# Convolution of a stage in two parts, batch statistics by ScalarE, one product of two blocks, and B and C by two transfers

## The chip, the core and the metric

The kernel runs on one core of a Trainium2 chip. TensorE (PE) multiplies matrices, VectorE (DVE) and GpSimd (POOL) do element-wise work, ScalarE (ACT) evaluates functions with a scale and a bias, SyncE (SP) issues transfers, and 16 DMA engines carry them. The metric is the device time of one execution in microseconds. Everything is in fp32.

## The reference, cut to what matters

The input x is 32 images of 96 channels, 56x56 each. It passes a ConvNeXt block (a depthwise 7x7 convolution, a LayerNorm, an MLP with GELU, a residual), then two Mamba layers over the 3136 tokens of an image, then a fused projection with a batch-norm over all images.

```python
# ConvNeXt block
h = conv_general_dilated(x, conv_w, padding=((3,3),(3,3)), feature_group_count=dim) + conv_b
...                                        # LayerNorm, w1, GELU, w2, scale
x = h + x
# a Mamba layer
dbl = xc @ xproj_w                         # dt (6), B (16), C (16) of each token
delta = softplus(dt @ dt_w + dt_b)         # 192 channels
dA  = exp(delta[..., None] * A)
dBx = delta[..., None] * Bm[:, :, None, :] * xc[..., None]
hstates = associative_scan(...)            # h[t] = dA[t] * h[t-1] + dBx[t], 192 x 16 rows
y = einsum('blds,bls->bld', hstates, Cm) + Dp * xc
y = y * silu(z)
...
# the end
out = einsum('oc,bchw->bohw', fus_w, cat) + fus_b
mu, var = out.mean((0, 2, 3)), out.var((0, 2, 3))
out = (out - mu) * rsqrt(var + EPS) * bn_g + bn_b
return out + residual
```

## The kernel before, in words

After a setup (to about 640 us) that also convolves the images of the first group of batches, a main loop runs 256 **stages**: 2 layers x 32 images x 4 chunks of 784 tokens (CH; half of it, 392, is HC). The order alternates the layers, so that a chunk of layer 2 follows soon after its layer 1. A final pass (from 17140 us) normalises and writes the output in 64 tiles.

A stage holds 192 x 16 scans of 784 tokens. They are done 128 rows at a time: 6 blocks j of 32 channels, times 4 groups g of 4 states, which gives 24 **steps**. A step consists of these instructions:

- ACT computes dA as an exp of the d tile (L805). A d tile has 128 rows: four copies of 32 channels of delta, brought by four transfers (load_d4, L684).
- PE spreads u (delta times xc) of a block over the 128 rows (spread, L820), and DVE multiplies it with B (w, L847). For the two "pooled" blocks, j = 2 and 5, POOL does this product instead (L831), from a tile us which transfers bring (L675).
- DVE runs the scan (L854); POOL multiplies with C (L858); PE adds up over the states (add_up, L885 and L891).
- Three times a stage DVE multiplies y with the gate (L872).

B and C come by transfer: the 32 rows of dbl go to a DRAM tile bd (dbl_out), and load_bc brings, for each group g, a tile bc of 128 partitions x 2 x 784: partitions 32s to 32s+31 hold 32 copies of the rows of B and C of state 4g+s. There are 8 such buffers, and a stage uses four.

All other work is cut into **pieces** that have a slot: a number whose whole part is the step after which the piece is put into the instruction stream, and whose fraction is its order there. A piece marked True runs within a step, between w and the scan. `prep` holds the pieces for the next stage (projections of the Mamba layer, dbl, softplus, the product u, loads of bc, d and us); its slots are counted for the coming stage and begin with negative ones. `post` ends the stage before: project (7.5), then two halves of move from PSUM (9 and 10), and in layer 2 the statistics for the batch-norm with DVE's bn_stats (stat, L760, at 13 within a step), after which the half is saved to o_d. `block0` is half a tile of the ConvNeXt block, and `conv` one channel pair of the depthwise convolution for a group of seven images: as a matrix product with a banded matrix over 112 rows (2 channels x 56), one product per horizontal tap. It is in 144 of the stages (stages 2 to 145). PSUM tiles from psum(0), psum(1) and psum(2) have one buffer each.

The order on every engine is written out by hand this way: each engine, and SP's queue of transfers too, executes its instructions in that order and waits at the head for what is not ready. The program's transfers share a few completion semaphores in turn, so that only some are under way at a time. The final pass reads the statistics back, merges them (bn_aggr, L967), and scales all tiles.

Of the kernel before, what the change touches and what calls it, by code (L numbers as in the profile page):

```python
# [34 lines left out]
F32 = mybir.dt.float32  # L35
I32 = mybir.dt.int32
AF = mybir.ActivationFunctionType
ALU = mybir.AluOpType
AX = mybir.AxisListType
# [4 lines left out]
L = H * W  # L44
C = 96
DIN = 192
NQ = 3
NS = 16
# [3 lines left out]
NCH = 4  # L52
CH = L // NCH
HC = CH // 2
# [7 lines left out]
def convnext_mamba_kernel(  # L62
# [31 lines left out]
    nc = tc.nc  # L94
    B = x.shape[0]

    dram = ctx.enter_context(tc.tile_pool(name="dram", bufs=1, space=DRAM))
# [3 lines left out]
    NB = 7  # L101
    b0 = B - 3 * NB if B > 3 * NB else B
    groups = [(0, b0)] + [(b, b + NB) for b in range(b0, B, NB)]
    conv_d = [
        dram.tile([C * H, (hi - lo) * W], F32, name=f"conv_d{lo}", tag=f"conv_d{lo}")
        for lo, hi in groups
    ]
    band_d = dram.tile([C // 2, 2 * H, 7 * 2 * H], F32, name="band_d")
    stats_d = dram.tile([C, B * NCH, 12], F32, name="stats_d")
    x1_d = [dram.tile([C, L], F32, name=f"x1_d{b}", tag=f"x1_d{b}") for b in range(B)]  # L110
    o_d = [dram.tile([C, L], F32, name=f"o_d{b}", tag=f"o_d{b}") for b in range(B)]

# [82 lines left out]
    for i in range(2):  # L195
# [12 lines left out]
        if i == 1:  # L208

            d["res"] = fw1  # L210
            for q in range(NQ):
                ps = sups.tile([128, 512], F32, name="ps", tag="nps")
# [5 lines left out]
                ps = sups.tile([128, 512], F32, name="ps", tag="nps")  # L218
# [29 lines left out]
    for k in range(2):  # L248
        t = const.tile([C + 1, 3 + CH], F32, name=f"hn{k}", tag=f"hn{k}")
        nc.vector.memset(t[C : C + 1, :], 1.0)  # L250
        hns.append(t)
        t = const.tile([C + 1, HC], F32, name=f"hz{k}", tag=f"hz{k}")
# [4 lines left out]
    R2 = 2 * H  # L257
    GB = (b0 + 1) // 2
    cb = const.tile([R2, C // 2], F32, name="cb")
    with tc.tile_pool(name="cc", bufs=1) as cc, tc.tile_pool(name="cx", bufs=3) as cx, tc.tile_pool(  # L260
        name="cp", bufs=6, space=PSUM
# [31 lines left out]
        for i in range(3):  # L293
            t = cc.tile([R2, 7, R2], F32, name=f"band{i}", tag=f"band{i}")
            nc.gpsimd.memset(t, 0.0)
            bands.append(t)
            t = cc.tile([R2, b0, W + 6], F32, name=f"xpad{i}", tag=f"xpad{i}")
            nc.gpsimd.memset(t, 0.0)
            xpads.append(t)
        for p in range(C // 2):  # L300
# [13 lines left out]
            for lo in range(0, b0, GB):  # L314
                n = min(GB, b0 - lo)
                ps = cps.tile([R2, GB * W], F32, name="ps")
                for dw in range(7):
                    nc.tensor.matmul(
                        ps[:, 0 : n * W], T[:, dw, :], xp[:, lo : lo + n, dw : dw + W],
                        start=(dw == 0), stop=(dw == 6),  # L320
# [3 lines left out]
                    bias=cb[:, p : p + 1],  # L324
# [4 lines left out]
    with ExitStack() as main:  # L329
        wp = main.enter_context(tc.tile_pool(name="wp", bufs=2))  # L330
# [12 lines left out]
        def tok(a):  # L343
            return slice(a * HC, (a + 1) * HC)
# [34 lines left out]
        batch_bias = {}  # L379
# [103 lines left out]
        xpad = wp.tile([R2, NB, W + 6], F32, name="xpad", tag="xpad", bufs=1)  # L483
        nc.vector.memset(xpad, 0.0)

        def conv(g, p):
            lo, hi = groups[g]
            v = {}

            def load():  # L490
                v["band"] = wp.tile([R2, 7, R2], F32, name="band", tag="band", bufs=1)
                nc.sync.dma_start(v["band"].rearrange("p k n -> p (k n)"), band_d[p])
                nc.sync.dma_start(
                    xpad[:, :, 3 : 3 + W],
                    x[lo:hi, 2 * p : 2 * p + 2, :].rearrange("b c (h w) -> (c h) b w", w=W),
                )

            def taps_(dws):
                def piece():
                    if dws[0] == 0:  # L500
                        v["ps"] = psum(2)
                    for dw in dws:
                        nc.tensor.matmul(  # L503
                            v["ps"][0:R2, 0 : NB * W], v["band"][:, dw, :],
                            xpad[:, :, dw : dw + W], start=(dw == 0), stop=(dw == 6),
                        )

                return piece

            def store():  # L510
                t = wp.tile([R2, HC], F32, name="sq", tag="sq", bufs=3)
                nc.scalar.activation(
                    t[:, 0 : NB * W], v["ps"][0:R2, 0 : NB * W], AF.Identity, bias=cb[:, p : p + 1]
                )
                nc.sync.dma_start(conv_d[g][p * R2 : (p + 1) * R2, :], t[:, 0 : NB * W])

            return [
                (-10, load), (7.7, taps_((0,))), (8.2, taps_((1,))), (8.6, taps_((2,))),
                (9.2, taps_((3,))), (9.6, taps_((4,))), (10.2, taps_((5,))), (10.4, taps_((6,))),
                (11.05, store),  # L520
            ]


# [6 lines left out]
        def prep(S):  # L530

            i, b, c = S.i, S.b, S.c
            d = lay[i]
            v = {}
# [81 lines left out]
            def load_bc(gs):  # L616
                def piece():
                    for g in gs:
                        t = wp.tile([128, 2, CH], F32, name="bc", tag="bc", bufs=8)
                        for s in range(4):  # L620
                            nc.sync.dma_start(
                                t[32 * s : 32 * s + 32],
                                v["bd"][4 * g + s :: NS, :].partition_broadcast(32),
                            )
                        S.bcs.append(t)

                return piece
# [20 lines left out]
                    nc.sync.dma_start(ddv[a], dl[rows(a)])  # L648
                S.d4 = []

            def product(q):
                def piece():
                    if q == 0:
                        S.u = wp.tile([128, NQ, HC], F32, name="u", tag="u", bufs=1)
                    nc.gpsimd.tensor_tensor(S.u[:, q], v["dl"][:, q], S.xc[:, q], ALU.mult)  # L655

                return piece

            def store_u(k):
                def piece():  # L660
                    j = POOLED[k]
                    if k == 0:
                        v["uu"] = bcd.tile([len(POOLED), 32, CH], F32, name="uu", tag="uu")
                        S.us = {}
                    for a in range(2):
                        r = 64 * a + 32 * (j % 2)
                        nc.sync.dma_start(v["uu"][k, :, tok(a)], S.u[r : r + 32, j // 2, :])

                return piece
# [10 lines left out]
            def load_d4(j):  # L680
# [11 lines left out]
            start = [  # L692
                (-18, load), (-12.9, center), (-11.9, square), (-11.8, halo), (-11.6, mean),
                (-11.2, root), (-9, True, norm),
            ]
            t = (-7.6, -7.5, -6.5, -6, 0, 0.1, 1, 2.3, 3.1, 3.4, 4)
            if S in (stages[2], stages[-1]):
# [5 lines left out]
                t = (12, 12, 13, 13, 14, 14, 15, 16, 17, 18, 19)  # L703
            elif S is stages[3]:
# [6 lines left out]
            t = [k + 0.1 for k in t]  # L711
# [6 lines left out]
                (t[6] + 0.2, silu("z", None)), (t[7], dbl), (t[8], dbl_out),  # L718
                (max(10.2, t[8] + 1.2), load_bc((0, 1))), (max(13.2, t[8] + 2.2), load_bc((2, 3))),
                (t[9], dt), (t[10], softplus),  # L720
                (max(16.2, t[10] + 1), product(0)), (max(17.2, t[10] + 2), product(1)),
                (max(18.3, t[10] + 3.1), store_u(0)), (25.2, product(2)), (26.3, store_u(1)),
                (max(17, t[10] + 2), load_d4(0)), (max(18, t[10] + 3), load_d4(1)),
                (max(20, t[10] + 3.2), load_u(0)), (23, load_d4(2)),
                (26, load_d4(3)), (32.9, load_u(1)), (30, load_d4(4)), (35, load_d4(5)),
# [2 lines left out]
        def post(S):  # L728


            i, b, c = S.i, S.b, S.c
            v = {}

            def project():
                v["ps"] = [psum(0), psum(1)]
                for a in range(2):
                    nc.tensor.matmul(
                        v["ps"][a][0:C, 0:HC], S.d["res"], S.seq[:, tok(a)],
                        start=True, stop=False,
                    )  # L740
                for q in range(NQ):
                    for a in range(2):
                        nc.tensor.matmul(
                            v["ps"][a][0:C, 0:HC], S.d["ow"][rows(a), q, :], S.z[rows(a), q, :],
                            start=False, stop=(q == NQ - 1),
                        )

            def move(a):
                def piece():
                    nc.scalar.activation(  # L750
                        S.seq[:, tok(a)], v["ps"][a][0:C, 0:HC], AF.Identity,
                        bias=batch_bias[b] if i == 1 else 0.0,
                    )

                return piece

            def stat():
                st = wp.tile([C, 2, 6], F32, name="stat", tag="stat", bufs=2)
                for a in range(2):
                    nc.vector.bn_stats(st[:, a, :], S.seq[:, tok(a)])  # L760
                nc.sync.dma_start(stats_d[:, b * NCH + c, :], st.rearrange("p a k -> p (a k)"))
                nc.sync.dma_start(o_d[b][:, c * CH : (c + 1) * CH], S.seq)
                del seqs[b, c]

            pieces = [(7.5, project), (9, move(0)), (10, move(1))]
            if i == 1:
                pieces.append((13, True, stat))
            return pieces


# [190 lines left out]


    mv = const.tile([C, 2], F32, name="mv")
    with tc.tile_pool(name="sp", bufs=1) as sp:
        stats = sp.tile([C, B * NCH * 2, 6], F32, name="stats")
        nc.sync.dma_start(stats.rearrange("p (n a) k -> p n (a k)", a=2), stats_d)
        nc.vector.bn_aggr(mv, stats)  # L967
    sc = const.tile([C, 1], F32, name="sc")
    nc.scalar.activation(sc, mv[:, 1:2], AF.Sqrt, bias=eps_c[0:C])
    nc.vector.reciprocal(sc, sc)  # L970
# [74 lines left out]
```

## Time and profile before

| | |
|---|---|
| time, median of 3 runs | 17518.44 us (17515.35 to 17520.57) |
| profiled execution | 17504.21 us, its span 17502.5 us |
| granted TensorE clock, mean | 0.936 |
| busy share of the span | DVE 92%, POOL 89%, PE 87%, ACT 64% |
| DMA | 2346.89 MB, mean 134 GB/s; 4096 transfers bc<-bd of 196 KB, 5.2 us to landing |
| first scan / end of the last scan | 641.8 us / 17128.3 us |

A row of a group gives the line, the engine and operation, the tile written and the tiles read, the shapes and the count; then busy time and the mean of one in ns; then the idle time of the engine ahead of it, and what ended that idle time. A window gives for a stretch of time its length and the busy time of each engine in it, with the number of instructions in brackets, then PE's granted clock, the mean busy share of the 16 DMA engines and the GB/s moved. A row of waits gives the engine and what it was about to do, what released it, the total, the number of times and the longest. Times of the DMA rows are medians from issue to landing.

### The profile page before, as it was taken

To read this page: it belongs to the slowest core of one execution; us is meant where nothing else is said; L and a number is where in the kernel's file an instruction comes from. 1 tells how busy PE (TensorE), PEld (TensorE's weight loads), DVE (VectorE), ACT (ScalarE), POOL (GpSimd) and SP (SyncE) were. 2 spreads that over 40 slices of the span, in tenths; PEclk is the share of its full clock that TensorE was granted. 3 is DMA by queue.
4 is the path that set the end of the run, shared out by engine and by line. 5 is a ranking of instruction groups with operands and counts; after the bars stand their busy time and mean duration, and the time that the engine had idled before them with its cause. 6 is when DMAs were issued, how large, how long until landed. Compare 5 with 4: busy or idle time off the path is not lost. (4 is left out here: it accounts for less than half of the span.)

```text
span 17502.5 us, 212206 instructions
## 1 busy us (share of the span) xinstructions
PE 15285.5 (87%) x65976; PEld 5191.4 (30%) x65976; DVE 16171.5 (92%) x12592; ACT 11224.1 (64%) x17479; POOL 15632.4 (89%) x8993
## 2 busy tenths in 40 slices
PE   7799999999999999999999988888888888888880
PEld 5233333333333333333333322222222222222220
DVE  7499999999999999999999999999999999999994
ACT  1566666666666666666666666666666666666653
POOL 0499999999999999999999999999999999999991
PEclk9799999999999999999999999999999999999985
DMA  4355555555555555555555555555555555555548
GB/s 102 87 139 138 138 135 136 140 139 139 138 135 138 137 140 138 134 137 137 139 139 134 136 126 128 128 125 125 126 129 127 125 126 126 129 127 124 126 116 273
DMA packets 1403525, 2346.89 MB, mean 134 GB/s; under 512 B 627654, under 2 KB 775154, under 8 KB 1402388
## 3 DMA queue, kind: packets, MB, share of 16 engines
q1 hardware_dynamic: 1395220, 2294.77, 53.1%
q10 hardware_dynamic: 7168, 38.54, 0.6%
q8 instruction: 520, 8.52, 0.2%
q14 instruction: 617, 5.05, 0.1%
HBM read 1929.50 MB, written 402.80 MB: 133 GB/s over the span
## 5 line engine op out<-in xcount | busy, mean ns | idle before, releaser
L858 POOL TENSOR_TENSOR da<-h,bc 128x784 f32<-128x784 f32 x6144 | 11295.8, 1863 | 884.9 <-DVE h L854 721.8
L854 DVE TENSOR_TENSOR_SCAN h<-da,st,w 128x784 f32<-128x784 f32 x3072 | 5662.4, 1843 | 314.3 <-ACT st L865 8.6
L891 PE MATMUL y<-da,ssum 128*32 128x392 f32 x24576 | 5086.0, 533 | 562.9 <-POOL da L858 561.2
L847 DVE TENSOR_TENSOR w<-w,bc 128x784 f32<-128x784 f32 x4096 | 3996.0, 976 | 311.0 <-PE w L820 139.5
L831 POOL TENSOR_TENSOR da<-us,bc 128x784 f32<-128x784 f32 x2048 | 3818.4, 1864 | 2.3 <-DMA us<-uu 2.3
L805 ACT ACTIVATE da<-d,A 128x784 f32<-128x784 f32 x4096 | 3753.9, 941 | 44.8 <-DMA d<-dd 28.6
L805 ACT ACTIVATE w<-d,A 128x784 f32<-128x784 f32 x2048 | 1879.6, 918 | 2659.7 <-DVE h L854 2403.2
L854 DVE TENSOR_TENSOR_SCAN h<-w,st,da 128x784 f32<-128x784 f32 x1536 | 2712.5, 1827 | 5.7 <-ACT st L865 4.6
L891 PEld LDWEIGHTS y<-da,ssum 128*32 128x32 f32 x24576 | 1097.3, 114 | 4106.8 <-issue 2359.5
L576 PE MATMUL ps<-hn,wx 97*64 97x392 f32 x12288 | 2260.4, 502 | 7.4 <-DVE hn L564 7.4
L854 DVE TENSOR_TENSOR_SCAN h<-da,w 128x784 f32<-128x784 f32 x1024 | 1826.4, 1784 | 106.7 <-ACT st L865 4.0
L820 PE MATMUL w<-u,sel 64*128 64x392 f32 x4096 | 1032.9, 583 | 719.0 <-DVE h L854 719.0
L655 POOL TENSOR_TENSOR u<-dl,xc 128x392 f32<-128x392 f32 x768 | 791.6, 1031 | 561.3 <-ACT dl L641 561.3
L576 PEld LDWEIGHTS ps<-hn,wx 97*64 97x64 f32 x12288 | 792.0, 136 | 1420.6 <-issue 1098.9
L885 PE MATMUL y<-xc,D 128*128 128x392 f32 x1536 | 796.8, 605 | 306.9 <-DVE z L872 305.2
L351 ACT ACT_TABLE_LOAD x759 | 973.8, 1283 | 14.7 <-PEq L1032 0.8
L854 DVE TENSOR_TENSOR_SCAN h<-w,da 128x784 f32<-128x784 f32 x512 | 872.2, 1766 | 0.0
L360 ACT ACTIVATE sq<-ps 96x392 f32<-96x392 f32 x768 | 340.6, 490 | 827.2 <-PE ps L355 529.7
L503 PE MATMUL ps<-xpad,band 112*112 112x392 f32 x2016 | 816.1, 520 | 0.0
L633 PE MATMUL ps<-dbl,dtw 6*64 6x392 f32 x3072 | 684.2, 509 | 100.3 <-ACT dbl L611 100.3
L820 PEld LDWEIGHTS w<-u,sel 64*128 64x128 f32 x4096 | 327.2, 196 | 1424.7 <-DVE h L854 1262.4
L865 ACT COPY st<-h 128x2 f32<-128x2 f32 x2304 | 417.5, 181 | 426.3 <-DVE h L854 424.9
(112 smaller groups left out, 14111.0 us busy)
## 6 DMA issues: line engine op xcount, KB each, us to landing
bc<-bd SPq DMA_DIRECT2D x4096, 196.0 KB, 5.2
d<-dd SPq DMA_DIRECT2D x6144, 98.0 KB, 2.6
us<-uu SPq DMA_DIRECT2D x2048, 98.0 KB, 2.2
dd<-dl SPq DMA_DIRECT2D x512, 294.0 KB, 3.8
uu<-u SPq DMA_DIRECT2D x1024, 49.0 KB, 1.6
band<-band_d SPq DMA_DIRECT2D x144, 343.0 KB, 7.4
cv<-conv_d SPq DMA_DIRECT2D x256, 147.0 KB, 2.4
xin<-in_x SPq DMA_DIRECT2D x128, 294.0 KB, 3.0
```

The costliest lines, as they stand in the source:

```text
L351: nc.scalar.preload_act_table_set("natural_log_exp_and_others")
L503: nc.tensor.matmul(v["ps"][0:R2, 0 : NB * W], v["band"][:, dw, :], xpad[:, :, dw : dw + W], start=(dw == 0), stop=(dw == 6),)
L576: nc.tensor.matmul(v["x", q][rows(a), 0:HC], weights[:, k, 64 * q : 64 * q + 64], v["hn"][:, o : o + HC], start=(k == 0), stop=(k == last),)
L655: nc.gpsimd.tensor_tensor(S.u[:, q], v["dl"][:, q], S.xc[:, q], ALU.mult)
L805: nc.scalar.activation(e, S.d4[j], AF.Exp, scale=S.d["A"][:, j, g : g + 1])
L820: nc.tensor.matmul(S.u4[:, 512 * a : 512 * a + HC], sel[rows(a), j % 2, :], S.u[rows(a), j // 2, :], start=True, stop=True,)
L831: nc.gpsimd.tensor_tensor(t, S.us[j], S.bcs[g][:, 0, :], ALU.mult)
L847: nc.vector.tensor_tensor(halves(db), S.u4.rearrange("p (a b) -> p a b", a=2)[:, :, 0:HC], halves(S.bcs[g][:, 0, :]), ALU.mult,)
L854: nc.vector.tensor_tensor_scan(ring[:, g, :], S.e.pop((j, g)), db, 0.0 if c == 0 else d["st"][:, j, g : g + 1], ALU.mult, ALU.add,)
L858: nc.gpsimd.tensor_tensor(da, ring[:, g, :], S.bcs[g][:, 1, :], ALU.mult)
L885: nc.tensor.matmul(S.y[:, 0:HC], S.d["D"][:, q, :], S.xc[:, q, :], start=True, stop=False)
L891: nc.tensor.matmul(S.y[r0 : r0 + 32, 0:HC], ssum, da[:, tok(a)], start=False, stop=(g == NG - 1),)
```

## The change

It has four parts.

1. **Convolution.** The seven images of a group are done in two parts: images 0 to 3 (224 columns) with their taps at slots 7.7 to 10.4, and images 4 to 6 (168 columns) with taps at 18.5 to 22.2. Each part has its own PSUM tile, its own copy by ACT and its own store (11.05 and 22.9). The load of the band and the padded images moves from slot -10 to -1.
2. **Statistics.** In layer 2, move accumulates the sum of the half while it copies it; at slots 17.2 and 18.2 ACT squares each half around its mean with an accumulator. DVE's bn_stats is gone; a stage stores 4 numbers per channel instead of 12. The save to o_d is a piece of its own at 12.9. Before the final pass ten DVE instructions take the place of bn_aggr.
3. **Product u.** The blocks q = 0 and 1 are multiplied in one instruction at slot 16.9 (128 x 784) instead of two at 16.2 and 17.2.
4. **B and C.** load_bc brings a group by two transfers, one for B and one for C, each over all 128 partitions, instead of four over 32 partitions each with both.

```diff
+        PARTS = (0, (NB + 1) // 2), ((NB + 1) // 2, NB)
...
-            def taps_(dws):
+            def tap(part, dw):
+                first, last = PARTS[part]
...
+                    nc.tensor.matmul(
+                        v["ps"][0:R2, 0 : (last - first) * W], v["band"][:, dw, :],
+                        xpad[:, first:last, dw : dw + W], start=(dw == 0), stop=(dw == 6),
+                    )
...
+            at = (7.7, 8.2, 8.6, 9.2, 9.6, 10.2, 10.4), (18.5, 18.6, 19.2, 20.2, 21.2, 21.3, 22.2)
             return [
-                (-10, load), (7.7, taps_((0,))), (8.2, taps_((1,))), (8.6, taps_((2,))),
-                (9.2, taps_((3,))), (9.6, taps_((4,))), (10.2, taps_((5,))), (10.4, taps_((6,))),
-                (11.05, store),
+                (-1, load), (11.05, store(0)), (22.9, store(1)),
+                *[(at[part][dw], tap(part, dw)) for part in range(2) for dw in range(7)],
             ]
...
                         t = wp.tile([128, 2, CH], F32, name="bc", tag="bc", bufs=8)
-                        for s in range(4):
+                        for k in range(2):
+                            src = v["bd"][NS * k + 4 * g : NS * k + 4 * g + 4, :]
                             nc.sync.dma_start(
-                                t[32 * s : 32 * s + 32],
-                                v["bd"][4 * g + s :: NS, :].partition_broadcast(32),
+                                t[:, k, :], src.unsqueeze(1).broadcast_to([4, 32, CH])
                             )
...
-                (max(16.2, t[10] + 1), product(0)), (max(17.2, t[10] + 2), product(1)),
-                (max(18.3, t[10] + 3.1), store_u(0)), (25.2, product(2)), (26.3, store_u(1)),
+                (max(16.9, t[10] + 1.5), product(0, 2)), (max(18.3, t[10] + 3.1), store_u(0)),
+                (25.2, product(2, 3)), (26.3, store_u(1)),
...
+                    nc.scalar.activation(
+                        S.seq[:, tok(a)], v["ps"][a][0:C, 0:HC], AF.Identity, bias=batch_bias[b],
+                        accum_out=v["st"][:, a : a + 1],
                     )
...
-                for a in range(2):
-                    nc.vector.bn_stats(st[:, a, :], S.seq[:, tok(a)])
...
+                    nc.scalar.activation(neg, v["st"][:, a : a + 1], AF.Copy, scale=-1.0 / HC)
+                    t = wp.tile([R2, HC], F32, name="sq", tag="sq", bufs=3)[0:C]
+                    nc.scalar.activation(
+                        t, S.seq[:, tok(a)], AF.Square, bias=neg,
+                        accum_out=v["st"][:, 2 + a : 3 + a],
+                    )
...
             if i == 1:
-                pieces.append((13, True, stat))
+                pieces += [(12.9, save), (17.2, stat(0)), (18.2, stat(1))]
```

## The prediction

> **What bounds the kernel now.** I read the busy shares first, then two windows far inside the loop, to see whether the engine that leads the average also leads in both kinds of stage.
>
> ```profile
> PE 15285.5 (87%) x65976; PEld 5191.4 (30%) x65976; DVE 16171.5 (92%) x12592; ACT 11224.1 (64%) x17479; POOL 15632.4 (89%) x8993
> ...
> 9000.00:10000.00 1000.00, 924.87 (x4035) 307.80 (x4036) 953.67 (x736) 675.08 (x1055) 952.93 (x548) 0.97 0.56 136
> 13000.00:14000.00 1000.00, 870.67 (x3802) 288.52 (x3802) 953.82 (x736) 665.37 (x1042) 950.24 (x546) 0.93 0.51 126
> ```
>
> The windows (PE, PEld, DVE, ACT, POOL busy us, clock, DMA share, GB/s) show DVE and POOL at 95% each in both kinds. The group rows and waits say which leads: POOL waits for DVE (721.8 us), DVE for POOL hardly at all.
>
> ```profile
> L858 POOL TENSOR_TENSOR da<-h,bc 128x784 f32<-128x784 f32 x6144 | 11295.8, 1863 | 884.9 <-DVE h L854 721.8
> L854 DVE TENSOR_TENSOR_SCAN h<-da,st,w 128x784 f32<-128x784 f32 x3072 | 5662.4, 1843 | 314.3 <-ACT st L865 8.6
> ...
> L847 DVE TENSOR_TENSOR w<-w,bc 128x784 f32<-128x784 f32 x4096 | 3996.0, 976 | 311.0 <-PE w L820 139.5
> ...
> L760 DVE BATCH_NORM_STATS2 stat<-seq 96x6 f32<-96x392 f32 x256 | 130.9, 551 | 3.7 <-ACT seq L750 3.7
> ...
> DVE w L847 <- PE w L820: 139.5, 122, 4.8
> DVE hz L419 <- ACT ps L372: 73.8, 69, 2.3
> ```
>
> So DVE sets the pace. First scan at 641.8 us, last scan's end at 17128.3: 16486.5 us, 64.4 us a stage, and 17502.5 - 16486.5 = 1016 us outside the loop. Its waits differ: in the 144 stages with a convolution nearly all is the product w at step 12 waiting for the spread, 111.9 us, as PE is late by the taps of steps 7 to 10; in the others hz waits for ScalarE at step 14, about 0.7 us a stage.
>
> The transfers bound nothing now, but come in bursts. SP's queue in one stage (first scan 5024.86, next stage's 5088.43):
>
> ```profile
> 5050.65 3.66 SPq L621 DMA_DIRECT2D bc<-bd  x8
> 5054.41 2.82 SPq L684 DMA_DIRECT2D d<-dd  x4
> ...
> 5058.76 4.34 SPq L621 DMA_DIRECT2D bc<-bd  x8
> ...
> 5064.94 9.78 SPq L684 DMA_DIRECT2D d<-dd  x8
> ...
> bc<-bd SPq DMA_DIRECT2D x4096, 196.0 KB, 5.2
> ```
>
> Sixteen transfers bring B and C of the next stage, from 26 us after the first scan; behind them in the same queue is the d tile that the next stage's first exp needs. Each lands in 5.2 us, so about 20 us are spare.
>
> **What the Trainium skill says.** "DMA: Bandwidth & Descriptors", "Why a DMA increments its semaphore by 16 and not by 1": the number of DMA engines of one transfer is the largest number up to 16 that divides the size of the slowest dimension above 1 of both sides; its "Rules for kernel authors" warn that an outermost dimension of c < 16 confines the transfer to c engines. The trace agrees where it has a case: wx<-in_taps (97 rows, prime) moves at 25 to 28 GB/s with a DMA share of a sixteenth. It has no outermost dimension of 4.
>
> "SBUF — State Buffer", "Door 1: The DMA port swizzle": partitions p and p+32 lie on one port, p+64 on another, so 32 rows reach half the ports. The trace agrees: bursts of 32-row transfers move 226 to 259 GB/s with all engines busy, the final pass with 96 rows 335.
>
> ```profile
> 5051.50:5059.00 7.50, 7.50 (x29) 2.72 (x28) 7.26 (x6) 5.10 (x10) 6.95 (x5) 1.00 1.02 233
> 5059.00:5063.00 4.00, 3.83 (x16) 1.19 (x14) 3.83 (x5) 2.96 (x8) 4.00 (x3) 1.00 1.04 259
> ...
> 32.00:33.00 1.00, 0.91 (x2) 0.40 (x2) 0.00 (x0) 0.00 (x0) 0.00 (x0) 1.00 0.07 28
> ...
> 17200.00:17400.00 200.00, 0.00 (x0) 0.00 (x0) 66.42 (x38) 63.20 (x38) 0.00 (x0) 0.50 1.02 335
> ```
>
> From these rows a 3136-byte packet takes about 3136 / 27 = 0.116 us on an engine alone, 3136 / (335/16.3) = 0.153 in the final pass, and 3136 / (233/16.3 to 259/16.6) = 0.20 to 0.22 where two engines press on one port.
>
> **The change, part by part.**
>
> *B and C by two transfers a group.* 16 DMAs a stage become 8 of 392 KB, 128 packets each. Read side [4 rows of bd][32 repeats][784], write side 128 partitions: the outermost sizes are 4 and 128, so by the rule four engines carry it, not sixteen. Each engine gets one state's 32 copies, 32 packets; the first two write partitions 0-31 and 32-63, step by step on the same port, the other two likewise. Price of a packet: 0.116 at best (nobody shares), 0.22 to 0.24 at worst (they always do); I take 0.21, the measured saturated case, as the partners start together. The four transfers of one load call then take 4 x 32 x 0.21 = 26.9 us where eight took some 8, and there are two calls. The chain of a stage: bc(0,1) starts at 26.2 (as now), 0.9 us to begin, 26.9, the d tile between them 1.0, bc(2,3) 26.9, d(0) of the next stage 1.0, landing 0.9, exp 0.93: 84.7 us to the next first scan, 78 if the first load starts as early as 20. I take 82 against 64.4. What is queued behind: all are SP transfers in one order, with few in flight at a time, so d(0), d(1), cv, uu and us come late one after another; ScalarE's exps wait for d, DVE's scans for those, POOL and PE for the scans. Cover: the 20 us spare above. It decides: the fixed terms are 26.2 + 0.9 + 1.0 + 1.0 + 0.9 + 0.93 = 30.9, so the loads are hidden as long as 256 packet times fit in 64.25 - 30.9 = 33.3 us, a packet up to 0.130 us. Eight fewer issues on SP (about 0.4 us each) cannot pay, SP being idle enough.
>
> *Statistics by ScalarE.* DVE loses 256 bn_stats of 0.551 us: 130.9 us. They stand between a w and its scan in 128 stages; the pair takes 1.83 us from w's start to the scan's start with them and less without, where the scan waits out w's end: 0.71 to 1.02 us a stage, 91 to 131 us. ScalarE gains two accumulator reads, two tiny Copies and two Squares of 392 (the LayerNorm square of that size takes 490 ns): about 2.1 us in a layer-2 stage, on an engine at 67%. Its own order is sensitive: hz waits for it at step 14, but the pieces stand at 17.2 and 18.2, behind that; cost 0 to 0.3 us, I take 0. The bn_aggr of 7.1 us becomes ten small DVE operations at the end: 0 to +5 us, I take +3.
>
> *Conv in two parts.* Taps of 392 columns (2016, 520 ns modelled; about 0.76 us with the weight load, as pairs) become 224 and 168 columns, 4032, the second half at steps 18 to 22. Some 7 x 0.76 x 3/7 = 2.3 us leave steps 7 to 10. The wait of w at step 12 (111.9 us) should go. What is late next is hz at step 14, which in the stages without taps already costs 0.7 us: 142 x 0.7 = 100 us may come back; net gain 12 to 112 us. PE does about 0.8 us more a conv stage (14 extra weight loads and starts), with PE at 92% in those windows; its cover is the idle time before L891, and if that goes, w at step 20 or y is late. Band and xpad are now loaded at step 23 for step 7: 8.0 us to land now, about 20 us of cover. The extra store and ACTIVATE are 0.6 us of ScalarE and one issue of 0.3 us on SP, hidden likewise.
>
> *u of two blocks at once.* Two products of 1.03 us become one of 1.86 on POOL: 0.13 us a stage saved where POOL waits for DVE: 0. *o_d saved at 12.9:* no wait on the path, 0.
>
> Sum without the transfers: -(91 to 131) - (12 to 112) + 3, so -100 to -240 us. With them: 256 x 82 + 1018 = 22,010 us; the gains disappear, since DVE then has time left over. The profiled execution is 17504.2 us, 14 below the median of the runs; against a difference of thousands I do not shift.
>
> **The rivals.**
>
> 1. *The transfers spread over all engines, or the four stay at the unshared price:* nothing in the trace shows an outermost 4, and partners that drift apart by four partitions no longer share a port. Below 0.130 us a packet everything hides and the DVE gain remains: 17504 - 150 = 17,350, range 17,290 to 17,420. This is the case on the other side, **faster**; against it stand the rule and the 97-row load that follows it.
> 2. *hz takes the place of the w wait and PE's new load eats the rest:* the transfers hidden, gain of about the bn_stats at most, and taps at 18 to 22 delay y: 17,480 to 17,550, no change.
> 3. *Half shared:* a packet of 0.135 to 0.18 us, e.g. 0.153 as in the final pass: 30.9 + 256 x 0.153 = 70.1 us a stage, 18,960; 17,600 to 19,800. For it: the reads are of few rows, and the other twelve engines add no pressure.
>
> **How the numbers follow.** Shared port, 0.18 to 0.24 us a packet: chance 0.58, 73 to 92 us a stage, 19,800 to 23,800, likeliest 22,000. Half shared: 0.14. These are the slower side, 0.72. Hidden: 0.22 faster; no change, within 0.2% (35 us, about what a measurement of this kernel can tell): 0.06. Both signs are held by the range, as 0.22 is more than may be left out: from 17,330 to 23,700. The likeliest case's own range is 19,800 to 23,800.
>
> **What would show it.** Right: a bc<-bd landing of 15 to 30 us instead of 5.2; in a window over the bc loads a DMA share near 0.25 and 60 to 80 GB/s instead of 1.02 and 233; DVE busy near 75%; long waits of an exp for d<-dd, once a stage, ending when d(0) lands; d<-dd landings of some 10 to 30 us. The steps for DVE: the bn_stats row gone, w's wait for the spread at step 12 gone. Wrong: a bc load at over 200 GB/s, or a stage of 64 us with bc landing late (then the cover was larger than my 20 us); and if a stage is long while bc lands within 8 us, the second tap group is to blame.

## The result and the profile after

The changed kernel takes 19033.2 us (median; 19015.8 to 19041.8) against 17516.9 us of the kernel before on the same chip: ratio 1.0863, interval 1.0846 to 1.0881. It is slower, as forecast, but by 1516 us, where 4500 had been forecast. The profiled execution has a span of 19025.4 us; the loop from the first scan (665.5) to the end of the last (18661.9) lasts 17996.4 us, or 70.3 us a stage instead of 64.4.

The busy shares and a window inside the loop, then the largest waits of ScalarE, DVE and POOL in the loop (columns as before):

```profile
PE 15962.4 (84%) x67992; PEld 5605.2 (29%) x67992; DVE 16063.8 (84%) x12345; ACT 11451.5 (60%) x18647; POOL 15614.6 (82%) x8737
...
9000.00:10000.00 1000.00, 894.48 (x3910) 316.58 (x3912) 872.63 (x667) 635.44 (x1050) 874.00 (x488) 0.93 0.44 126
```

```profile
ACT da L836 <- DMA d<-dd: 1864.2, 250, 31.5
...
DVE h L885 <- ACT st L896: 932.0, 192, 29.0
...
DVE w L878 <- PE w L851: 609.6, 417, 8.5
...
DVE h L885 <- ACT da L836: 270.2, 62, 21.6
```

No engine is the bound any more: DVE's work has even shrunk by 107.7 us, but it is busy 87% of the window where it was 95%. Once a stage the exp for the first scan waits for its d tile (250 times, 1864.2 us in all, 7.5 us each). Before the change that wait was:

```profile
ACT da L805 <- DMA d<-dd: 28.6, 3, 11.1
```

The scan behind it waits with it, 932.0 + 270.2 us; that the first is put down to st only says that the copy of the state stood behind the late exp in ScalarE's queue. The third row is for the most part the echo: at step 4 w waits for the spread (466 of the 609.6 us), since pieces of ScalarE that PE needs stood behind the same exp.

SP's queue in one such stage (first scan 5592.34, the next stage's 5662.74), and three stretches of it as windows:

```profile
5621.31 3.38 SPq L633 DMA_DIRECT2D bc<-bd  x4
5624.79 6.54 SPq L697 DMA_DIRECT2D d<-dd  x4
5631.44 0.51 SPq L522 DMA_DIRECT2D conv_d<-sq  x1
5634.38 9.11 SPq L633 DMA_DIRECT2D bc<-bd  x4
5643.59 17.16 SPq L697 DMA_DIRECT2D d<-dd  x8
```

```profile
5634.00:5641.00 7.00, 5.47 (x24) 1.84 (x22) 6.76 (x8) 6.92 (x12) 6.27 (x4) 1.00 0.26 103
5643.00:5647.00 4.00, 4.00 (x16) 1.37 (x12) 3.70 (x4) 1.11 (x3) 4.00 (x3) 1.00 0.26 102
5654.00:5656.00 2.00, 2.00 (x12) 0.58 (x11) 2.00 (x2) 1.18 (x2) 2.00 (x2) 1.00 0.26 99
```

A DMA share of 0.26 is four engines of sixteen, at about 102 GB/s where before 233 to 259 were moved. The eight d transfers take 17.16 us to issue instead of 9.78. Three of the eight wait for a bc transfer to land, as these rows of SP's waits show, before and after (768 is three times in each of 256 stages); the waits are fewer and longer now.

```profile
SPq L684 <- DMA bc<-bd: 738.5, 1393, 1.5
SPq L697 <- DMA bc<-bd: 2657.3, 768, 4.8
```

The exp of the first scan starts at 5661.62 us, after 5.11 us of waiting. What it waits for here is not the issue. The trace also marks when each engine of a transfer reports its end: four for a bc transfer, sixteen for one of d. The four transfers of d(0), the first half of the eight, were issued by 5650.52, and twelve engines of each had reported by 5652.57. The other four reported between 5659.53 and 5661.44, right behind the last bc transfer (5659.30 to 5660.43). So it was in all stages: in the median of stages 4 to 253 the last report of d(0) comes 10.3 us after the last of the twelve early ones (0.4 before the change), and the exp starts 0.1 us after the last. Before the change d(0) was complete 12.1 us ahead of its exp. A tile carried by sixteen engines is as late as its share on the four that the loads keep busy.

### The profile page after: what moved, and what is told of

It is laid out like the page before. It is cut to its first block, busy times and chain, and to the rows that moved or that the text cites. A ratio compares the mean times of both kernels' runs of the same rounds, so it can differ in the third digit from the quotient of the medians.

```text
span 19025.4 us, 212510 instructions
## 1 busy us (share of the span) xinstructions
PE 15962.4 (84%) x67992; PEld 5605.2 (29%) x67992; DVE 16063.8 (84%) x12345; ACT 11451.5 (60%) x18647; POOL 15614.6 (82%) x8737
## 5 line engine op out<-in xcount | busy, mean ns | idle before, releaser
L922 PE MATMUL y<-da,ssum 128*32 128x392 f32 x24576 | 5150.2, 543 | 390.6 <-POOL da L889 388.6
L836 ACT ACTIVATE da<-d,A 128x784 f32<-128x784 f32 x4096 | 3760.0, 942 | 1915.2 <-DMA d<-dd 1864.2
L878 DVE TENSOR_TENSOR w<-w,bc 128x784 f32<-128x784 f32 x4096 | 3996.2, 976 | 743.9 <-PE w L851 609.6
L587 PE MATMUL ps<-hn,wx 97*64 97x392 f32 x12288 | 2550.5, 555 | 672.1 <-ACT sq L519 664.7
L587 PEld LDWEIGHTS ps<-hn,wx 97*64 97x64 f32 x12288 | 869.2, 149 | 2261.8 <-issue 1311.8
L587 PE MATMUL ps<-hn,inw 97*64 97x392 f32 x3072 | 776.1, 655 | 583.7 <-ACT xc L600 583.7
L666 POOL TENSOR_TENSOR u<-dl,xc 128x784 f32<-128x784 f32 (+1 forms) x512 | 734.7, 1435 | 565.7 <-ACT dl L652 565.7
L506 PE MATMUL ps<-xpad,band 112*112 112x224 f32 (+1 forms) x4032 | 1003.4, 359 | 0.0
L506 PEld LDWEIGHTS ps<-xpad,band 112*112 112x112 f32 x4032 | 584.4, 175 | 831.9 <-issue 792.4
```

The source lines that it names most:

```text
L506: nc.tensor.matmul(v["ps"][0:R2, 0 : (last - first) * W], v["band"][:, dw, :], xpad[:, first:last, dw : dw + W], start=(dw == 0), stop=(dw ...
L587: nc.tensor.matmul(v["x", q][rows(a), 0:HC], weights[:, k, 64 * q : 64 * q + 64], v["hn"][:, o : o + HC], start=(k == 0), stop=(k == last),)
L666: nc.gpsimd.tensor_tensor(S.u[:, lo:hi], v["dl"][:, lo:hi], S.xc[:, lo:hi], ALU.mult)
L836: nc.scalar.activation(e, S.d4[j], AF.Exp, scale=S.d["A"][:, j, g : g + 1])
L878: nc.vector.tensor_tensor(halves(db), S.u4.rearrange("p (a b) -> p a b", a=2)[:, :, 0:HC], halves(S.bcs[g][:, 0, :]), ALU.mult,)
L922: nc.tensor.matmul(S.y[r0 : r0 + 32, 0:HC], ssum, da[:, tok(a)], start=False, stop=(g == NG - 1),)
```

## The experiments

Times are medians, each compared with the kernel before on the same chip; ratios have their 95% interval. "Theory A" is the chain of the prediction: four-engine loads, and what stands behind them in the queue is late.

**Loads put back, and loads alone.** One kernel has everything changed but load_bc, the other nothing but load_bc:

```diff
# after_bc4, against the changed kernel; before_bc2 is the reverse, in the kernel before
-                        for k in range(2):
-                            src = v["bd"][NS * k + 4 * g : NS * k + 4 * g + 4, :]
...
+                        for s in range(4):
+                            nc.sync.dma_start(
+                                t[32 * s : 32 * s + 32],
+                                v["bd"][4 * g + s :: NS, :].partition_broadcast(32),
+                            )
```

> The changed kernel with load_bc as before (four transfers a group of 32 partitions each). Theory A, four-engine loads hold the next stage's first exp: all of the loss goes and the DVE gain of the other three parts is left, 17290 to 17420 us, stage 63.3 to 64.0 us, no long wait of da for d<-dd. Theory B, the second tap group and ScalarE's statistics cost it on PE and ACT: the loss stays, 18700 to 19100 us, w at step 4 still waits 1.5 us a stage for the spread.

> The kernel before with only load_bc changed to two transfers a group. Theory A: the whole loss appears without the other parts, stage 69 to 71 us, 18700 to 19200 us, da waits 5 to 7 us a stage for d<-dd, DMA share 0.26 and about 102 GB/s while the loads run. Theory B: 17450 to 17600 us.

Measured: after_bc4 17441.9 us against 17512.1, ratio 0.9960 (0.9945 to 0.9975). before_bc2 19560.2 us, ratio 1.1172 (1.1154 to 1.1191). So the loads are the whole loss: theory B (the second group of taps) is out, though after_bc4 misses the range of theory A by 22 us: the other parts bring less than expected. da's wait for d is 27.9 us in the first and 2109.9 us in the second:

```profile
ACT da L805 <- DMA d<-dd: 2109.9, 246, 31.4
```

before_bc2 loses 527 us more than the changed kernel, beyond what was expected. Its stages with a convolution take 73.5 us, those without 70.2; in the changed kernel both take 70. In before_bc2 the band (343 KB) and the padded images are still loaded at slot -10, which is between the loads of B and C and d(0), and those two issues hold SP some 4.5 us there. In the changed kernel that load stands at slot -1, behind d(0). 3.5 us in each of 142 stages are 500 us, so the difference lies in the stages that have this load. That its move makes it is argued from size and place; it was not tried by itself. If so, the move is worth something only because another part of the change had made that place critical.

**How much of it: half and three quarters.**

```diff
# after_half; after_3q has "g < 3"
+                        if g < 2:
                             for k in range(2):
...
+                        else:
+                            for s in range(4):
...
```

> The changed kernel with two-transfer loads for groups 0 and 1 only, groups 2 and 3 by four transfers as before. Theory A: the stream shrinks by about 12 us, twice what the stage is late, so all of the loss goes: 17300 to 17500 us. A cost in proportion to the four-engine transfers (theory C) would leave half of it: 18100 to 18300 us.

> The changed kernel with two-transfer loads for groups 0, 1 and 2, four-transfer ones for group 3. Half of the groups cost nothing, all of them 6 us a stage. If the stream is a chain with a cover (theory A), one group less takes about 2 x 32 x 0.126 = 8 us of four-engine time, less some 2 us for its normal transfers: 6 us, about what the stage is late, so 17430 to 17700 us. If the cost beyond half is in proportion to the transfers, half of the 6 us stays: 18100 to 18350 us.

Measured: 17464.9 us, ratio 0.9973 (0.9963 to 0.9984), and 17980.9 us, ratio 1.0263 (1.0246 to 1.0280). By mean stage with a convolution (stages 4 to 145): no group in the new form 63.92 us, two groups 63.89, three 66.11, four 70.03. A cost in proportion to the transfers is refuted: the first two groups cost nothing. The step from two to three groups is 2.2 us, that from three to four 3.9, so the cover ends within the third. The reports of d(0) agree: it is complete 12.1 us ahead of its exp before the change, still 1.9 us in after_half, and too late in after_3q, where the exp waits 4.2 us. There the last four engines report only 1.6 us after the other twelve; it is the issue of d(0) that comes late, 3.4 us before the exp. So slow loads delay a tile in two ways, by its share on their engines and by its place in SP's queue. after_3q falls between the two expectations: I had taken 6 us for a group and an end of the cover after the third.

**The same transfers at another place in the queue.**

```diff
# after_early
-                (max(10.2, t[8] + 1.2), load_bc((0, 1))), (max(13.2, t[8] + 2.2), load_bc((2, 3))),
+                (max(4.5, t[8] + 1.2), load_bc((0, 1))), (max(11.5, t[8] + 2.2), load_bc((2, 3))),
# after_late, against the changed kernel
-                (max(13.2, t[8] + 2.2), load_bc((2, 3))),
+                (max(18.6, t[8] + 3.3), load_bc((2, 3))),
```

> The changed kernel, its two-transfer loads issued earlier: groups 0 and 1 at slot 4.5 instead of 10.2, groups 2 and 3 at 11.5 instead of 13.2. The same transfers on the same four engines. Theory A: the stream of some 39 us starts about 12 us earlier and ends before the first exp of the next stage needs its d tile: stage 64 to 65.5 us, 17350 to 17750 us, us may come some us late for POOL. Theory C, the transfers cost by their traffic (engines or ports shared with d and us) wherever they stand: 18700 to 19100 us.

> The changed kernel with the two-transfer load of groups 2 and 3 at slot 18.6 instead of 13.2, so behind the next stage's d(0) and d(1) in SP's queue; nothing else. Theory A (what stands behind the four-engine loads is late): only groups 0 and 1 stand ahead of d(0), some 16 us of stream, so the first scan is no longer late; bc of groups 2 and 3 is first needed at step 2 and lands about then, cv and us come late: stage 64 to 66.5 us, 17400 to 18000 us. Theory C (the traffic itself costs, wherever it stands): 18900 to 19200 us.

Measured: 19421.8 us, ratio 1.1095 (1.1078 to 1.1111), and 19200.3 us, ratio 1.0961 (1.0946 to 1.0976). Both expectations for theory A were missed; the second time lies at the upper edge of theory C's, the first 320 us above it. The exp's wait for d fell from 1864.2 us to 560.3 us (early) and 57.1 us (late). Other waits took its place, first in after_early, then in after_late:

```profile
PE ps L355 <- DMA seq<-x_d: 1491.6, 125, 13.9
POOL da L862 <- DMA us<-uu: 1472.4, 227, 9.4
```

```profile
POOL da L862 <- DMA us<-uu: 1246.7, 146, 18.4
...
POOL da L862 <- DMA d<-dd: 551.4, 63, 11.8
```

Before the change POOL waited 2.3 us for us in all, and seq was there 8.1 us (median) before PE took it. Early, the loads of groups 0 and 1 stand ahead of us(1) and, in every second stage, of seq, the input that the next stage of layer 1 takes its LayerNorm from. Twelve engines report seq 3.6 us after its issue, the other four 10.5 us later, and PE starts 0.14 us after these; ScalarE and hz on DVE follow (hz waits 1837.0 us in the whole run). Those stages last 77.1 us, the others 66.2, so seq, which no expectation had named, makes most of the loss. Late, the loads of groups 2 and 3 stand ahead of us(0), whose last four engines report 10.3 us after the other twelve; POOL stands still, and DVE's scans wait for POOL (1164.0 us). The expectations had named a late us and put it at little. Neither place was free: the queue has consumers all through the stage, and a load call of some 16 us hits another one. What these two leave open is whether the loads delay what stands behind them in their own queue, or all transfers alike. The next kernel asks that.

**Another queue.**

```diff
# after_actq
-                            nc.sync.dma_start(
+                            nc.scalar.dma_start(
                                 t[:, k, :], src.unsqueeze(1).broadcast_to([4, 32, CH])
                             )
```

> The changed kernel with the two-transfer loads of B and C issued from ScalarE's queue instead of SP's, at the same slots; they take the same four engines. Theory A1, the loss comes from standing behind the loads in SP's queue: d and us no longer wait behind them, 17450 to 17800 us, with some us a stage of ScalarE held at its own issues (8 of about 0.5 us). Theory A2, the loss comes from what all transfers share (those under way at a time, and the four engines): da still waits for d<-dd by several us a stage, or ScalarE is held at the issues instead, 18500 to 19600 us.

Measured: 20279.3 us, ratio 1.1581 (1.1563 to 1.1598), worse than both expectations. Theory A1 was right about d: the exp's wait for it is 76.5 us in all, and the last four engines report d(0) 3.4 us after the other twelve, not 10.3. So it is behind the loads in one queue that d came late. But now ScalarE and SP wait elsewhere. Two waits of ScalarE in the loop, and one of SP:

```profile
ACT da L836 <- issue: 1570.8, 329, 15.9
ACT da L836 <- DMA bc<-bd: 1209.5, 112, 17.9
```

```profile
SPq L697 <- DMA bc<-bd: 5093.4, 1043, 12.2
```

ScalarE now holds its own exps at the issues: in one stage the last four issues take from 39.2 to 48.9 us after the first scan, the third and the fourth 4.1 us each. There are two reasons. Eight completion semaphores serve both queues in turn, so an issue can wait for a transfer of the other queue that still holds its own; SP's row shows it. The longest issues wait for something else: in all 261 that took over 3 us the semaphore was free when they began, and they ended 0.4 us (median) after the landing of the load four before, as if the queue took no more than four such loads at a time. What each of the two costs was not measured apart.

**The other parts, one by one.** before_stat has only the statistics, before_conv only the convolution in two parts; their edits are those parts of the change's diff.

> The kernel before with only the statistics moved to ScalarE. Theory D, DVE's time alone counts: 91 to 131 us less, 17380 to 17420 us. Theory E, hz's wait for ScalarE and PE at step 14 and w's for the spread grow by part of what DVE saves: 20 to 60 us less, 17450 to 17490 us, the waits of hz and w longer in the odd (layer 2) stages.

> The kernel before with only the convolution in two parts and its load at slot -1. Theory D: the wait of w at step 12 goes and nothing takes its place, 100 us less, 17400 to 17430 us. Theory E: a new wait of w at step 0 (spread behind the last taps) and hz take half or more of it: 17460 to 17510 us.

Measured: before_stat 17429.1 us, ratio 0.9954 (0.9941 to 0.9966); before_conv 17495.3 us, ratio 0.9989 (0.9981 to 0.9997). The statistics bring 86 us, 9 us short of theory D's range, and unevenly: the stages that held bn_stats fall from 64.61 to 63.65 us where there is a convolution, from 64.33 to 64.02 only where there is none; the stages between them rise from 63.90 to 64.16 and go from 64.22 to 64.23. The convolution in parts brings 20 us, theory E. Its wait did move, but not to hz, which stays (73.8 us before, 77.9 now, in the stages without taps). The 111.9 us of w at step 12 became 10.9 us at step 12 and 85.2 us at step 0: the last tap, at slot 22.2, stands on PE ahead of the spread for the next stage. Together (after_bc4) they bring 70 us, less than the statistics alone, within what the intervals leave.

**A faster version.**

```diff
# best, against after_bc4
+        last = {}
...
-        def conv(g, p):
+        def conv(g, p, real=True):
             lo, hi = groups[g]
-            v = {}
+            v = last
...
+            if not real:
+                return [(k, tap(0, dw)) for dw, k in enumerate((7.7, 8.2, 8.6, 9.2, 9.6, 10.2, 10.4))]
-            at = ... (18.5, 18.6, 19.2, 20.2, 21.2, 21.3, 22.2)
+            at = ... (18.5, 18.6, 19.2, 20.2, 21.2, 21.3, 21.4)
...
+            elif m >= len(convs) + 2:
+                put(m, conv(*convs[-1], real=False))
# stat_fill: before_stat with the same extra products, 392 columns wide, and no split
```

> The changed kernel with four-transfer loads of B and C, the last tap at 21.4 instead of 22.2, and in the stages without a convolution seven extra products of the first part's shape at the same slots, whose result is not read: they only keep PE's granted clock up. If hz at step 14 waits there because PE runs at half clock in steps 10 to 12, that wait (about 1 us a stage) goes: 60 to 100 us less than with the loads alone put back; the tap moved earlier takes 0 to 70 us (w at step 0). 17270 to 17400 us. If the clock is not the cause, hz waits as before and the time is 17400 to 17450 us.

> The kernel before with the statistics by ScalarE, and in the stages without a convolution the seven products of 392 columns at their usual slots with a result that is not read. If the clock in steps 10 to 12 is the cause of hz's wait, about 0.9 us in each of some 110 stages goes against the statistics alone: 17310 to 17370 us. The conv stages keep their wait of w at step 12.

Measured: best 17301.0 us against 17515.2, ratio 0.9877 (0.9862 to 0.9892), so 1.2% less than the kernel before; stat_fill 17416.5 us, ratio 0.9945 (0.9933 to 0.9958). Steps 11 to 13 of a stage without a convolution, first in after_bc4, then in best:

```profile
13487.30:13496.00 8.70, 7.17 (x16) 2.71 (x12) 8.43 (x8) 4.74 (x8) 8.34 (x5) 0.61 1.01 231
```

```profile
13399.40:13408.00 8.60, 7.80 (x32) 3.10 (x29) 8.33 (x8) 5.28 (x9) 8.25 (x5) 1.00 1.00 227
```

PE's granted clock, the third number from the end, is 0.61 in the first and 1.00 in the second. Over steps 10 to 13 of all stages from 148 to 253 it is 0.74 and 1.00. The Trainium skill, "TensorE: Matmul & The Clock Gate", "HAM oscillation — how this bites in real kernels", gives the rule to leave PE no idle gaps over some 3.4 us. Here less was enough: just ahead of the slowed stretch PE is idle for 2.75 us and, after 0.85 us of work, for another 1.53 us, and at the end of this its clock falls to half for 6.8 us. Ahead of the two windows PE is busy 0.54 of 3.30 us in after_bc4 and 3.22 of 3.40 in best. DVE's waits over the whole run, after_bc4 and then best:

```profile
DVE hz L419 <- ACT ps L372: 217.0, 84, 16.4
DVE w L878 <- PE w L851: 124.5, 167, 4.8
```

```profile
DVE hz L419 <- ACT ps L372: 115.9, 8, 16.4
DVE w L883 <- PE w L856: 87.8, 103, 4.8
```

The 101.0 us of hz in stages without a convolution are gone (the eight waits left lie elsewhere), and w at step 0 fell from 73.9 to 37.4 us with the earlier tap. The extra products could only delay what stands behind them on PE, so it is the clock that brings hz forward; stat_fill, where they are the only addition to before_stat, loses the wait of hz as well. But there 80.7 us of w at step 12 took its place in the same stages (7.4 us in best), so it misses its expectation: seven products of the full width delay the spread as the taps do. best is 115 us ahead of stat_fill. It has the split of the convolution, which these waits speak for, but also the earlier tap and the other parts of the change, which were not taken apart.

## Why the prediction was right and wrong

*Four engines:* right. The DMA share of 0.26 is what the Trainium skill's rule gives ("DMA: Bandwidth & Descriptors", "Why a DMA increments its semaphore by 16 and not by 1"); the trace before had no case of it, and this one agrees.

*The packet's price, 0.21 us:* this step failed. From the windows a packet takes 3136 / (103 / (16 x 0.26)) = 0.127 us, near the price of an engine alone. That partners would press on one port all the time ("SBUF — State Buffer", "Door 1: The DMA port swizzle") was inferred from where four engines would write; the measured rate shows no such loss. Why not (engines that drift apart, or a port that two of them do not fill) was not tested. A load call needs 4 x 32 x 0.127 = 16.3 us, not 26.9.

*The fixed terms, 30.9 us, and the cover up to 0.130 us a packet:* this failed the other way. With 0.127 they give 30.9 + 256 x 0.127 = 63.4 us, hidden; measured was 70.3. In the stage shown the first load went out 29.0 us after the first scan and not 26.2 (27.5 in the median of all stages). From the first bc issue to the exp of the next stage are 5661.62 - 5621.31 = 40.3 us, where 256 packets account for 32.5. The sum had charged 3.8 us for everything else in that stretch, and it was 7.8. The tile of d between the two calls is not the reason: on the four engines its end comes 1.0 us after that of the load ahead, as charged, however long its issues took. The excess lies for the most part in the first, the second and the sixth load, which took 2.5, 1.5 and 1.0 us more than the price; why stays open. So the sum was too long by 256 x (0.21 - 0.127) = 21.2 us, and too short by 2.8 at the start and 4.0 in the stream: 84.7 - 21.2 + 6.8 = 70.3, against 70.4 in this stage. The 20 us of cover were counted from the issue of d(0); from its landing they were 12.1.

*Sign and size:* the chain of waits was right, an exp that waits for d(0) behind the loads once a stage, and the size was wrong. The sign was in part luck: with the measured price of a packet the same sum would have said hidden, and only the second error, of opposite sign, makes it slower. The time fell in the range of the third rival (18,960 us), but not for its reason; a packet took less than it assumed, and 0.127 lies in the first rival's region, where all should hide. Of the signs named, the DMA share came as said; the rate was 99 to 103 GB/s and not 60 to 80, DVE's share 84% and not 75%, and a load was complete 15.1 us after its issue in the median, at the low end of the 15 to 30 named.

*The other parts:* bn_stats, 91 to 131 us forecast, 86 measured, just below. The convolution, 12 to 112 us forecast, 20 measured, with the right thought (a next wait takes the place) and the wrong wait: w at step 0, not hz. ScalarE's added work showed no cost. The product and the save of o_d were not measured by themselves.

## What to carry to other kernels

Fewer and larger transfers are not cheaper as such: look at the outermost size of both sides, because it can shrink the number of engines, and then ask what stands behind the slow transfer in its queue. A transfer over all engines is done when its slowest engine is. A cover is used up before it hurts: half of the slow loads cost nothing here and the last quarter cost 4 us a stage, so a hidden cost needs its threshold, counted from when a tile lands and not from when its transfer is issued. When an edit removes a wait, look for the next one on the same engine, and for an idle PE whose clock falls.

## What the runs showed of the hardware

Transfers with outermost sizes of 4 and 128 kept a share of 0.26 of the sixteen engines busy and moved 99 to 103 GB/s, 0.127 us for a 3136-byte packet. A transfer over sixteen engines issued behind them in the same queue was done on twelve engines 2.3 us after its last issue and on the other four 10.3 us later (the d(0) of the changed kernel, medians); with the loads in another queue the last four were 3.4 us behind. And work that is not needed can pay: seven unread products in each of 110 stages raised the clock in steps 11 to 13 from 0.61 to 1.00 in the stage shown and took away the waits of hz, about 1 us a stage.
